# Fixed first tiles of the routed experts, expert bias added at evacuation, and an ordered entry of one-head attention in a graph network kernel

## The chip, the cores and the metric

The kernel runs on one core of a Trainium2 chip. The metric is the device time of the program in microseconds (us). The kernel before takes 2925.66 us, the median of three runs (2923.8, 2925.66 and 2935.31).

## The reference

A graph of 2708 nodes with 256 features passes four layers; each is an attention over the neighbours of the graph (`_gnn`), then a feed-forward part (`_ffn`), both on normalized features and added to `x`.

```
x = x + _L0_gnn_ref(_layernorm(x), adj, ...);  x = x + _L0_ffn_ref(_layernorm(x), ...)
x = x + _L1_gnn_ref(_layernorm(x), adj, ...);  x = x + _L1_ffn_ref(_layernorm(x), ...)
x = x + _L2_gnn_ref(_layernorm(x), adj, ...);  x = x + _L2_ffn_ref(_layernorm(x), ...)
x = x + _L3_gnn_ref(_layernorm(x), adj, ...);  x = x + _L3_ffn_ref(_layernorm(x), ...)
```

Four of these eight parts matter here. `_L1_ffn` sends every node to one of 8 experts (top-1); hidden width 1024:

```
H = gelu(x @ W1 + b1)
probs = softmax(H @ Wg + bg);  assign = argmax(probs)
out[n] = probs[n, assign[n]] * (H[n] @ Wd[assign[n]] + bd[assign[n]])
```

`_L2_gnn` and `_L3_gnn` are attentions with one head (the second adds an elu, the first a bias `W_b`):

```
Wh = h @ W (+ W_b);  f1 = Wh @ a1;  f2 = Wh @ a2
e = leaky_relu(f1[:, None] + f2[None, :], 0.2), -9e15 where adj is 0
out = softmax(e, axis=1) @ Wh
```

`_L2_ffn` is a decoder block: causal attention, then 8 experts of which each node takes two (top-2), `(silu(x @ w1.T) * (x @ w3.T)) @ w2.T`, hidden width 682.

## The kernel before, in words

Nodes lie in 22 tiles of 128 rows (the last has 20), and `X` keeps all of them in on-chip memory. Stages follow one another; most take blocks of 512 nodes, six in all, the last of 148. The order within a stage comes from the order of the code on each engine's queue, and from `issue_after`, which ties an instruction to stand behind another.

**Top-1 experts, `top1_ffn` (L851).** A hidden loop over the six blocks makes H transposed (`hidden`, L900: matmuls at L905, Gelu on ACT), `gate` (L926) makes the routing scores and ranks each node within its expert (`Routing.chunk`, L1322; ranks at L1351, scatter of node numbers into slots by POOL at L1372), and `store` (L912) turns H back to rows (transposes L920, copies L921 by DVE and ACT) and stores each tile to DRAM on SP's queue (L924). `route.finish` (L1382) works out which expert owns which slot. A slot is a tile of 128 places of one expert: in the worst case 29, "usual" 26; slots above the usual number stand under a branch (`others`, L1449). For each slot, SP reads a row number into a register and loads the slot's node numbers, one column of 128 x 4 bytes (L1474); DVE casts them (L962); POOL gathers the rows of H (L964); PE transposes them (L978; copies L979 by DVE and ACT); PE multiplies by the expert's weights, whose number it has read into a register (16 matmuls, L985), and adds the expert's bias by a matmul with K = 8 and a one-hot column (`route.hot`, two instructions, L988); ACT or DVE by turns copies the result (L992), and POOL scatters it to DRAM (L1495). Ahead of slot 0, `prepare` computes the routing weights (`route.weights`) and folds the weights of the coming attention g2 (`Head`, L1033: loads on POOL's queue, products on DVE; L1037, L1045, L1047).

**One-head attention, `gat_single` (L1055)**, runs twice: g2 behind the top-1 experts, g3 behind the decoder. Its entry adds what the experts sent to `X` (`Routing.combine`, a generator by blocks of tiles, DVE), takes mean and variance of each tile (`Stats.sums`, L136: bn_stats and bn_aggr on DVE at L144 and L145, Sqrt on ACT at L146), the reciprocal (L149), normalizes (L108, DVE), transposes on PE (L1098), copies (L1102, ACT), multiplies by W (L123, PE), and forms the exponentials of the scores (L1108, L1109, ACT), the scaled rows V (L1111 ACT and L1113 DVE by turns), a sum of features (L1114, DVE) and the row `big_p` (L1120, ACT). Blocks come in the order 0, 1, 2, then 3 to 5; statistics in three groups: block 0, blocks 1 and 2, blocks 3 to 5. In g2 22 adds of the bias to `X` on POOL (L1149) follow. Then the main loop runs over groups of 768 nodes and 22 tiles j: Relu on ACT (L668), mask on DVE (L669), matmuls (L1168).

**Decoder experts, `experts` (L1761)**, works as the top-1 experts do, with 47 usual slots, of a worst case of 50. SP loads 128 x 258 numbers per slot (f, with the node number in two last columns), again behind a register read; `where` (L1476) works out where a result goes. `inverse_root` (L301), four Newton steps on DVE, serves the decoder's norms.

## Time and profile before

| | before |
|---|---|
| median of three runs | 2925.66 us |
| the profiled execution, its own time | 2935.18 us |
| its span, 33103 instructions | 2933.1 us |
| mean granted TensorE clock | 0.943 |
| busy: PE, DVE, ACT, POOL | 2676.8, 1458.5, 1046.9, 367.2 us |
| hidden loop of the top-1 experts | about 1092 to 1218 us |
| top-1 slots, 26 | 1240.4 to 1376.4 us |
| entry of g2, from its first add to `X` to the main loop | 1384.7 to 1441.9 us |
| decoder slots, 47 | 2198.9 to 2605.7 us |
| entry of g3, likewise | 2613.9 to 2679.4 us |

The span runs from the first to the last instruction of one profiled execution; the execution's own time holds 2.1 us more. Busy time is the sum of an engine's instructions, so an engine at 91% still has waits. Where lines of a view are shown below, "L1168" is line 1168 of the kernel, "acc<-V,e" is output and inputs, "x16" is how many instructions the row puts together, and "<-" in brackets says what ended the idle time before a row.

### The profile page before, as it was taken

How to read it: one execution, taken by the hardware profiler on the slowest of the kernel's cores; microseconds unless marked ns; L12 is line 12 of the kernel's file. 1: busy time of each engine (PE TensorE's matmuls, PEld its weight loads, DVE VectorE, ACT ScalarE, POOL GpSimd, SP SyncE). 2: the span in 40 equal slices, each digit the busy share in tenths (PEclk: the TensorE clock that was granted, in tenths of full speed). 3: DMA queues.
4: the chain of work that ended last, by engine and by line, in shares of the span. 5: the costliest groups of instructions: out<-in, count | busy, mean ns of one | idle time of the engine just before them, and what ended most of it. 6: DMA issues, size and time to landing. Idle time of an engine off the chain costs nothing.

```text
span 2933.1 us, 33103 instructions
## 1 busy us (share of the span) xinstructions
PE 2676.8 (91%) x11945; PEld 1633.7 (56%) x11945; DVE 1458.5 (50%) x3089; ACT 1046.9 (36%) x1605; POOL 367.2 (13%) x464
## 2 busy tenths in 40 slices
PE   6999989799999979797899899999969999969998
PEld 4667646563333325486688433333336676747885
DVE  7743358344777773422644455465543222245455
ACT  3344433225665633211543223233312221224453
POOL 0000012100000001232200123233321111110002
PEclk9999999698999989899999999899959999989999
DMA  8899210000000023443200100002031101041001
GB/s 297 283 293 312 85 64 1 8 0 1 1 1 1 1 85 133 115 130 103 77 1 1 33 22 17 15 2 89 15 109 33 33 30 33 29 151 40 1 1 39
DMA packets 110323, 196.66 MB, mean 67 GB/s; under 512 B 12154, under 2 KB 71034, under 8 KB 107454
## 3 DMA queue, kind: packets, MB, share of 16 engines
q1 hardware_dynamic: 89816, 147.89, 15.6%
q0 software_dynamic: 13360, 38.73, 4.2%
q10 hardware_dynamic: 6986, 7.91, 0.9%
q8 instruction: 100, 1.64, 0.2%
q14 instruction: 61, 0.50, 0.1%
HBM read 134.78 MB, written 59.71 MB: 66 GB/s over the span
## 4 chain that ended last, share of the span: by engine, by line
PE 74%; DVE 10%; DMA 5%; issue 5%; ACT 3%; POOL 2%; ACTq 0%; POOLq 0%; SPq 0%; DVEq 0%
PE acc L1168 15%; PE acc L774 8%; PE acc L278 7%; PE den L782 4%; PE po L1826 4%; PE po L1656 4%; PE sc L1641 3%; PE score L267 3%; DMA f<-hs 3%; PE h L905 3%; PE h L1794 3%; PE pv L123 2%; PE sc L1619 2%; PE po L123 2%; PE y L985 1%
## 5 line engine op out<-in xcount | busy, mean ns | idle before, releaser
L669 DVE SCALAR_TENSOR_TENSOR e<-e,mask 128x768 f32<-128x768 f32 (+2 forms) x264 | 409.5, 1566 | 312.9 <-ACT e L668 312.7
L668 ACT ACTIVATE e<-big_p,minus_one,ratio 128x768 f32<-128x768 f32 (+2 forms) x264 | 394.8, 1513 | 362.8 <-PE acc L1168 229.4
L1168 PE MATMUL acc<-V,e 128*128 128x257 f32 (+1 forms) x1936 | 433.5, 383 | 4.5 <-DVE e L669 2.8
L1168 PEld LDWEIGHTS acc<-V,e 128*128 128x128 f32 (+1 forms) x1936 | 352.2, 186 | 85.8 <-issue 32.1
L774 PE MATMUL acc<-e,V 128*64 128x512 f32 (+1 forms) x1056 | 249.7, 550 | 4.1 <-DVE e L669 4.1
L1794 PE MATMUL h<-w,ft 128*128 x752 | 233.9, 453 | 0.5 <-ACT ft L1783 0.5
L278 PE MATMUL acc<-F,e 128*128 128x257 f32 x968 | 226.3, 384 | 3.0 <-DVE e L275 2.6
L278 PEld LDWEIGHTS acc<-F,e 128*128 128x128 f32 x968 | 173.4, 185 | 67.0 <-DVE e L275 28.4
L774 PEld LDWEIGHTS acc<-e,V 128*64 128x64 f32 x1056 | 95.4, 137 | 180.6 <-issue 158.1
L1641 PE MATMUL sc<-qt,kt 64*128 64x512 f32 (+4 forms) x656 | 185.7, 538 | 4.3 <-ACT e L1651 2.6
L1651 ACT ACTIVATE e<-sc 128x1024 f32<-128x1024 f32 (+4 forms) x140 | 102.7, 760 | 201.1 <-PE sc L1641 177.7
L1794 PEld LDWEIGHTS h<-w,ft 128*128 128x128 f32 x752 | 136.4, 191 | 56.9 <-issue 1.6
L275 DVE TENSOR_TENSOR e<-e,mask 128x512 f32<-128x512 f32 (+2 forms) x132 | 80.5, 625 | 149.2 <-ACT e L269 147.4
L1659 DVE TENSOR_TENSOR sum<-sum,e 128x1024 f32<-128x1024 f32 (+4 forms) x102 | 104.1, 1020 | 97.7 <-ACT e L1651 94.1
L269 ACT ACTIVATE e<-score 128x512 f32<-128x512 f32 (+2 forms) x132 | 69.7, 544 | 179.8 <-PE score L267 153.1
L1656 PE MATMUL po<-e,V 128*64 128x512 f32 (+5 forms) x560 | 119.1, 509 | 14.9 <-ACT e L1651 8.9
L1826 PE MATMUL po<-w,ht 114*128 x564 | 131.2, 382 | 0.9 <-DVE ht L1819 0.9
L1641 PEld LDWEIGHTS sc<-qt,kt 64*128 64x128 f32 x656 | 71.3, 199 | 95.3 <-issue 81.5
L782 PE MATMUL den<-e,low 128*3 128x512 f32 (+1 forms) x1056 | 123.1, 542 | 0.0
L1826 PEld LDWEIGHTS po<-w,ht 114*128 114x128 f32 x564 | 107.9, 191 | 23.1 <-DVE ht L1819 8.2
L1485 DVE TENSOR_SCALAR second<-f,down 128x1 f32<-128x1 f32 x47 | 9.9, 213 | 219.1 <-DMA f<-hs 219.1
L267 PE MATMUL score<-QK 128*128 128x512 f32 (+2 forms) x264 | 112.8, 558 | 1.2 <-ACT e L269 0.7
(600 smaller groups left out, 3554.8 us busy)
## 6 DMA issues: line engine op xcount, KB each, us to landing
row<-in_adj SPq DMA_DIRECT2D x21, 1354.0 KB
raw<-in_adjT SPq DMA_DIRECT2D x35, 768.0 KB
hs<-zero SPq DMA_DIRECT2D x8, 2838.0 KB
hidden<-hr SPq DMA_DIRECT2D x21, 512.0 KB
wd<-in_f_wd SPq DMA_DIRECT2D x8, 1024.0 KB
kept<-mask SPq DMA_DIRECT2D x21, 338.5 KB
mask<-kept SPq DMA_DIRECT2D x21, 338.5 KB
f<-hs SPq DMA_DIRECT2D x47, 129.0 KB
```

The costliest lines, as they stand in the source:

```text
L123: self.nc.tensor.matmul(out, lhsT[:, c, :], rhs[:, c, :], start=first and c == 0, stop=last and c == n - 1)
L267: nc.tensor.matmul(ps[:r, :iw], QK[:, 0, span(j)], QK[:, 1, i0 : i0 + iw], start=True, stop=True)
L278: nc.tensor.matmul(acc[k][:ri], e[:r, k * P : k * P + ri], F[:r, j, :], start=j == 0, stop=j == NT - 1)
L668: nc.scalar.activation(v, big_p[:, i], AF.Relu, bias=net.minus_one, scale=ratio)
L669: nc.vector.scalar_tensor_tensor(v, v, 1.0, net.mask[:, j, i], ALU.add, ALU.mult)
L774: nc.tensor.matmul(acc[n][half, :iw], V[:, j, h, :], e[:, k, i0 : i0 + iw], start=j == 0, stop=j == NT - 1)
L782: nc.tensor.matmul(den[g : g + Q, :iw], low[:, j, h, Q - 1 - q : 2 * Q - 1 - q], e[:, k, i0 : i0 + iw], start=False, stop=j == NT - 1 and ...
L1168: nc.tensor.matmul(acc[k][:ri], e[:, k * P : k * P + ri], V[:, j, :], start=j == 0, stop=j == NT - 1)
L1641: nc.tensor.matmul(ps[:r, g, o:iw], kt[b, span(j)], qt[b, o:iw], start=True, stop=True)
L1656: nc.tensor.matmul(po[b, o:iw], V[:r, j, g, :], e[:r, g, o:iw], start=j == 0, stop=j == last)
L1794: last = nc.tensor.matmul(halves[s, n][:, q, :HALF], fts[s][:, c, :], weights.w13[n][:, bass.ds(es[s], 1), c, q * HALF : (q + 1) * HALF], ...
L1826: last = nc.tensor.matmul(po, ht[:KP, k, :], w2[:KP, bass.ds(es[s], 1), k, :], start=k == 0, stop=k == KC - 1)
```

## The change

It has three parts.

1. *Top-1 experts.* The first tile of each expert is always slot 0 to 7, so those slots need no register; the further tiles follow, and the routing's helper arrays shrink by 8 tiles. One load (`load_first`) brings the node numbers of the first 8 slots, and the other columns are loaded up front. The bias of the experts is broadcast to all partitions by a load of 1 MB on ACT's queue, and DVE adds it while it copies the result; for slots from 8 on, DVE reads the expert's number into a register. `store` of the last-but-one block is kept until the last block has passed its gate; each half of a tile has its own buffer, in a ring of three shared with `q4`, and its own store. `Head` moves from ahead of slot 0 to behind the add of slot 3, its loads to ACT's queue.
2. *Entry of one-head attention.* `turn` puts DVE's steps in an order written out: block 0 alone, then block 1, then further blocks two by two. ACT takes Sqrt for blocks 0 and 1 alone, ahead of the first exponential; the other roots are Newton steps on DVE (`Stats.newton`), now three and not four, which holds for `inverse_root` everywhere. The copy of `ft` becomes two ACT copies that also sum (`accum_out`), in place of DVE's sum at L1114. V is scaled by ACT in blocks 0 to 3, by DVE in blocks 4 and 5. The bias adds of g2 go into the main loop, behind the mask of j = 3.
3. *Decoder experts.* Slots 0 to 7 are fixed likewise, and the routing's `owners`, the weights and `place` follow the first slot's gate.

```diff
-    def sums(self, t0, t1):
+    def sums(self, t0, t1, root=True):
...
-            nc.vector.bn_aggr(self.mv[:r, t, :], st[:r])
-        nc.scalar.activation(self.sd[:, g], self.mv[:, g, 1], AF.Sqrt, bias=net.ln_eps)
+            last = nc.vector.bn_aggr(self.mv[:r, t, :], st[:r])
+        if root:
+            self.root = nc.scalar.activation(self.sd[:, g], self.mv[:, g, 1], AF.Sqrt, bias=net.ln_eps)
+        return last
...
     def roots(self, t0, t1):
-        self.net.nc.vector.reciprocal(self.rstd[:, t0:t1], self.sd[:, t0:t1])
+        return self.net.nc.vector.reciprocal(self.rstd[:, t0:t1], self.sd[:, t0:t1])
...
+    def newton(self, pool, t0, t1):
+        return inverse_root(self.net, pool, self.mv[:, t0:t1, 1], 1.0, LN_EPS, "nr", self.rstd[:, t0:t1])
...
-    for _ in range(4):
+    for _ in range(3):
         nc.vector.scalar_tensor_tensor(t, y, -0.5, y, ALU.mult, ALU.mult)
         nc.vector.tensor_tensor(t, t, x, ALU.mult)
-        nc.vector.scalar_tensor_tensor(y, t, 1.5, y, ALU.add, ALU.mult)
-    return y
+        last = nc.vector.scalar_tensor_tensor(y, t, 1.5, y, ALU.add, ALU.mult)
+    return y if out is None else last
...
-        bd = big.tile([E, D], F32, name="bd")
-        nc.gpsimd.dma_start(bd, a["f1_bd"])
...
-                    hr = rp.tile([P, 2, 512], F32, name="hr", bufs=2)
                     for n, half in enumerate(halves):
+                        hr = rp.tile([P, 512], F32, name="hr", bufs=3)
...
-                    nc.sync.dma_start(rows_of[span(t), :], hr[:r].rearrange("p n m -> p (n m)"))
+                        nc.sync.dma_start(rows_of[span(t), n * 512 : (n + 1) * 512], hr[:r])
...
-            blocks = chunks(512)
+            blocks, kept = chunks(512), []
             ft = features(tiles_of(*blocks[0]))
             for n, (n0, nw) in enumerate(blocks):
                 its = tiles_of(n0, nw)
@@ -947,102 +954,132 @@
                 if n + 1 < len(blocks):
                     ft = features(tiles_of(*blocks[n + 1]))
                 gate(its, halves, nw)
-                store(its, halves)
+                kept.append((its, halves))
+                if n + 2 != len(blocks):
+                    for k in kept:
+                        store(*k)
+                    kept.clear()
...
+            bd = sp.tile([P, E, D], F32, name="bd", bufs=1)
+            nc.scalar.dma_start(bd.rearrange("p e d -> p (e d)"), a["f1_bd"].rearrange("e d -> (e d)").partition_broadcast(P))
...
+            def numbers(group):
+                g = slice(group[0], group[-1] + 1)
+                nc.vector.tensor_copy(number[:, g], node[:, g])
...
+            def places(group):
+                g = slice(group[0], group[-1] + 1)
+                at = sp.tile([P, E], F32, name="at", bufs=2)[:, : len(group)]
+                nc.vector.tensor_tensor(at, node[:, g], route.taken[:, g], ALU.mult)
+                nc.vector.tensor_tensor(to[:, g], at, route.spare[:, g], ALU.add)
...
-                    nc.tensor.matmul(
-                        ps, ht[:, c // 4, c % 4, :], wd[:, bass.ds(experts[s], 1), c, :], start=c == 0, stop=False
-                    )
-                last = nc.tensor.matmul(
-                    ps, route.hot[:E, s : s + 1].to_broadcast([E, P]), bd, start=False, stop=True
-                )
...
+            def expert(engine, s):
+                if s < E:
+                    return slice(s, s + 1)
+                return bass.ds(engine.value_load(route.expert[0:1, s : s + 1], min_val=0, max_val=E - 1), 1)
...
+            route.load_first(node[:, :E])
+            for s in range(E, usual):
+                route.load(s, node[:, s : s + 1])
+            numbers(groups[0])
+            for s in range(4):
+                fetch(s)
+            ready = transposes(0)
+            route.owners()
+            places(groups[0])
+            route.weights(one)
+            heads = []
...
                     with tc.issue_after(last.ins) if last else nullcontext():
-                        experts[s] = nc.tensor.value_load(route.expert[0:1, s : s + 1], min_val=0, max_val=E - 1)
+                        e = expert(nc.tensor, s)
                     this = ready
                     if s + 1 < s1:
                         ready = transposes(s + 1)
-                    last = results(s, *this)
+                    ps = py.tile([P, D], F32, name="y")
+                    for c in range(KC):
+                        last = nc.tensor.matmul(
+                            ps, this[:, c // 4, c % 4, :], wd[:, e, c, :], start=c == 0, stop=c == KC - 1
+                        )
+                    with tc.issue_after(added.ins) if added else nullcontext():
+                        e = expert(nc.vector, s)
+                    y = sp.tile([P, D], F32, name="ys")
+                    added = nc.vector.tensor_tensor(y, ps, bd[:, e, :].rearrange("p e d -> p (e d)"), ALU.add)
+                    route.send(to[:, s : s + 1], y)
+                    with tc.issue_after(added.ins):
+                        for g in groups[1:]:
+                            if s + 6 == g[0]:
+                                numbers(g)
+                                places(g)
+                        if s == 3:
+                            heads.append(Head(net, prep, one, "g2", True, nc.scalar))
                     if s + 4 < s1:
                         fetch(s + 4)
-            heads = []
...
-            through(0, route.usual, prepare)
+            through(0, usual, ready)
...
-        nc.gpsimd.dma_start(w[:, :, :D], a[f"{key}_w"].rearrange("(c p) m -> p c m", p=P))
-        av = net.load_rows(work, a[f"{key}_a"], 2 * D, "av")
+        engine.dma_start(w[:, :, :D], a[f"{key}_w"].rearrange("(c p) m -> p c m", p=P))
...
-                    nc.scalar.copy(ft[:, :, k * P : k * P + pw], ps[:, :, :pw])
+                    for c in range(2):
+                        nc.scalar.activation(
+                            ft[:, c, k * P : k * P + pw],
+                            ps[:, c, :pw],
+                            AF.Copy,
+                            accum_out=parts[:, 2 * n + k // 2, c : c + 1],
+                        )
...
-                        nc.scalar.activation(low, pv[:r, D:], AF.Exp, scale=SLOPE)
+                        with tc.issue_after(ln.root.ins) if t == 0 else nullcontext():
+                            nc.scalar.activation(low, pv[:r, D:], AF.Exp, scale=SLOPE)
                         nc.scalar.activation(ratio[:r, t : t + 1], pv[:r, D:], AF.Exp, scale=1.0 - SLOPE)
-                        if m:
+                        if n < 4:
                             nc.scalar.activation(V[:r, t, :D], pv[:r, :D], AF.Copy, scale=low)
                         else:
-                            nc.vector.tensor_scalar(V[:r, t, :D], pv[:r, :D], low, None, ALU.mult)
-                nc.vector.tensor_reduce(parts[:, n, :], ft[:, :, :nw], AX.X, ALU.add)
+                            with tc.issue_after(last.ins):
+                                nc.vector.tensor_scalar(V[:r, t, :D], pv[:r, :D], low, None, ALU.mult)
...
-            next(rest)
-            stats(0, 0)
-            next(rest)
-            norm(0)
+            def tiles(n0, n1):
+                return tiles_of(*blocks[n0])[0], tiles_of(*blocks[n1])[-1] + 1
+            last = None
+            def turn(step, *args, **kw):
+                nonlocal last
+                with tc.issue_after(last.ins) if last else nullcontext():
+                    new = step(*args, **kw)
+                last = new or last
+            def add():
+                return next(rest, None)
+            turn(add)
+            turn(ln.sums, *tiles(0, 0))
+            turn(add)
+            turn(ln.roots, *tiles(0, 0))
+            turn(norm, 0)
+            turn(ln.sums, *tiles(1, 1))
+            turn(add)
             project(0)
-            next(rest)
-            stats(1, 2)
-            next(rest)
-            norm(1)
+            turn(ln.roots, *tiles(1, 1))
+            turn(norm, 1)
             project(1)
-            next(rest)
-            norm(2)
-            project(2)
-            next(rest)
-            stats(3, 5)
-            for n in range(3, 6):
-                norm(n)
+            turn(ln.sums, *tiles(2, 2), root=False)
+            turn(add)
+            turn(ln.sums, *tiles(3, 3), root=False)
+            turn(ln.newton, small, *tiles(2, 3))
+            for n in (2, 3):
+                turn(norm, n)
                 project(n)
-            if bias:
-                for t in range(NT):
-                    r = rows(t)
-                    nc.gpsimd.tensor_tensor(X[:r, t, :], X[:r, t, :], bias[:r], ALU.add)
+            turn(add)
+            turn(add)
+            turn(ln.sums, *tiles(4, 5), root=False)
+            turn(ln.newton, small, *tiles(4, 5))
+            for n in (4, 5):
+                turn(norm, n)
+            for n in (4, 5):
+                project(n)
             nc.vector.tensor_reduce(fsum, parts.rearrange("p n c -> p c n"), AX.X, ALU.add)
...
-                gat_pairs(net, e, j, i0, iw, big_p, ratio[:, j : j + 1])
+                masked = gat_pairs(net, e, j, i0, iw, big_p, ratio[:, j : j + 1])
+                if bias is not None and i0 == 0 and j == 3:
+                    late = small.tile([P, D], F32, name="late", bufs=1)
+                    with tc.issue_after(masked.ins):
+                        nc.vector.tensor_copy(late, bias)
+                    for t in range(NT):
+                        r = rows(t)
+                        nc.gpsimd.tensor_tensor(X[:r, t, :], X[:r, t, :], late[:r], ALU.add)
...
-            nc.vector.tensor_scalar(n, ps, float(P - 1), None, ALU.add)
+            nc.vector.tensor_scalar(n, ps, 1.0, -1.0, ALU.max, ALU.add)
...
+        if s < self.E:
+            self.loaded = sync.dma_start(f, self.hs[s * CAP : s * CAP + P, :])
+            return
...
+    def load_first(self, f):
+        self.loaded = self.net.nc.sync.dma_start(
+            f, self.hs.rearrange("(e c) d -> c (e d)", e=self.E)[:P, :]
+        )
...
+            if s < E:
+                es[s] = slice(s, s + 1)
+                return
...
             for s in range(s0, min(s0 + 4, s1)):
                 fetch(s)
-            if prepare:
-                route.owners()
             front(s0)
-            if prepare:
-                prepare()
...
             gate(s0)
+            if s0 == 0:
+                route.owners()
+            place(s0)
+            place(s0 + 1)
+            if s0 == 0:
+                shares()
```

## The prediction

> **What bounds the kernel now.** I read the page's engine totals and slices first, then the chain that ended last, then that chain for the stages that the change touches, then windows of the entries.
>
> ```profile
> PE 74%; DVE 10%; DMA 5%; issue 5%; ACT 3%; POOL 2%; ACTq 0%; POOLq 0%; SPq 0%; DVEq 0%
> ```
>
> Over the span PE is 91% busy and carries 74% of the chain: a saving counts where PE has less to do, or where PE waits. The chain for 1160 to 1290 us shows both kinds:
>
> ```profile
> 1217.70 0.56 DVE hr L921
> 1219.72 0.61 PE rank L1351 x2
> ...
> 1223.68 4.20 DMA fnodes<-ftag,fto
> 1228.25 0.53 issue
> 1228.78 0.77 POOL g2w L1037
> 1229.55 2.71 DMA g2bv<-in_g_b
> 1235.65 0.61 DVE bt L1047
> 1236.35 4.04 DMA hr<-hidden,number
> 1240.41 1.94 PE ht L978 x8
> ```
>
> Columns are start, length, what. Between the last hidden block and the first slot of the top-1 experts PE waits about 20 us for a relay: ranks, scatter of node numbers, a DVE that stands for g2's weights, gather. Then PE alone sets the pace:
>
> ```profile
> 1280.26 1.02 PE ht L978 x8
> 1281.29 3.46 PE y L985 x16
> 1284.74 0.62 PE y L988 x2
> 1285.36 1.02 PE ht L978 x8
> ```
>
> A slot is 1.02 + 3.46 + 0.62 = 5.10 us; 26 of them run from 1240.4 to 1376.4. The two entries of one-head attention are mixed. Columns: stretch, length, PE, PEld, DVE, ACT, POOL busy (instructions), granted clock, DMA share, GB/s.
>
> ```profile
> 1384.70:1391.70 7.00, 0.00 (x0) 0.02 (x1) 6.99 (x23) 0.30 (x1) 0.11 (x1) 0.50 0.72 227
> 1391.70:1400.70 9.00, 8.94 (x28) 6.14 (x28) 9.00 (x28) 4.40 (x14) 2.87 (x4) 0.71 0.00 1
> 1400.70:1405.00 4.30, 0.44 (x3) 0.20 (x2) 4.30 (x10) 3.43 (x4) 1.97 (x1) 0.85 0.08 10
> 1405.00:1414.00 9.00, 8.69 (x26) 5.98 (x27) 8.91 (x22) 2.99 (x12) 5.81 (x8) 0.69 0.47 150
> 1414.00:1420.70 6.70, 6.32 (x29) 4.65 (x28) 6.30 (x21) 6.01 (x14) 2.47 (x4) 1.00 0.48 150
> ```
> ```profile
> 2636.00:2640.00 4.00, 1.39 (x6) 0.51 (x4) 4.00 (x14) 3.68 (x7) 0.00 (x0) 0.92 1.04 406
> 2654.20:2657.20 3.00, 0.06 (x1) 0.06 (x2) 2.23 (x12) 2.18 (x3) 0.00 (x0) 0.87 0.01 3
> 2657.20:2666.30 9.10, 9.10 (x28) 6.85 (x29) 4.88 (x12) 4.23 (x13) 0.00 (x0) 0.67 0.00 0
> 2666.30:2673.00 6.70, 6.41 (x30) 4.69 (x29) 2.10 (x3) 3.43 (x14) 0.00 (x0) 1.00 0.01 2
> ```
>
> PE waits 7 us for block 0, about 4 us for block 1 (behind DVE), and in g3 again 3 us for block 3. A block costs 6.7 us at clock 1.00 and 9.0 at 0.7.
>
> **1. Expert bias.** The matmul pair at L988 goes: 26 x 0.62 = **16.1 us**, all on the chain. In its place DVE adds a broadcast bias while it evacuates, in every slot (before: copies of 0.42 us on DVE, 0.37 on ACT, by turns), and reads the expert number into a register in 18 slots. No DVE register load is in the trace. Nearest is SP's: its node loads come every 1.09 us with 0.33 of that the issue, so 0.76 us; DVE then does 0.69 (ht copy) + 0.42 + 0.76 = 1.9 us per 4.48-us slot. It binds only above 4.48 - 1.11 - about 0.5 of waiting = 2.9 us. Behind the load stand the bias add and the next ht copy, for which PE waits. I take nothing; bounds 0 to 3 us lost. A gain is excluded, since nothing leaves PE but L988. POOL has 2.56 us per slot (two indirect DMAs at 0.97 to 0.99, two gaps of 0.30), also below 4.48.
>
> **2. Dispatch.** Stores of block 4 are put behind block 5's gate, so ranks come earlier by that block's four tiles of transposes and copies: their two groups take PE and the copies about 6.4 us, from the stretch between the last hidden matmul and L1351. The scatter then lands near 1222.5 instead of 1227.9. What is late next is SP: ten half-row stores in a ring of three, about 1.07 us each, the last near 1225.3, and the node load stands behind them in SP's queue. It is now one load of 128 x 8 numbers. The Trainium skill, "DMA: Bandwidth & Descriptors", rules for kernel authors, warns that a strided last dimension becomes one descriptor per element: 1024 pieces where one column had 128, a reason against. The trace prices such pieces: from 1228.2 to 1240.3 us the hardware queue moved 1160 small packets in 4.7% of 16 engines' time, 12.1 x 0.047 = 0.57 us. So 1024 cost about 0.5 us beyond the landing time; as an upper bound I take the issues of the eight column loads that it replaces, 8 x 0.33 = 2.6. I take 0.5, the row of the same pieces. The 1 MB bias broadcast, moved to ACT's queue here, could hold it up by 0 to 3 us (1 MB at the 340 GB/s of nearby slices); I take 1. So the numbers arrive near 1228.5, DVE's weights (softmax behind an Exp table load of 1.28 at 1219.44) end near 1228.8, number near 1229; first gather to first PE took 5.4 us (1235.03 to 1240.41), so PE starts near 1235: **5 us** (2 to 8).
>
> The 4.60-us DVE wait for g2's bias goes. Head's folding, about 4.0 us of DVE, moves to behind slot 3's add with its DMAs on ACT's queue. There the ht copy of slot 5 is done some 5.3 us after that add and PE needs it at 5.5: free, but close. Without this cover up to 4 us once.
>
> **3. Hidden loop.** Each tile's two halves share a ring of three buffers. A half's copy 0.69, store issue 0.33, landing about 2 and hand-overs 0.2 make 3.2 us per three halves, 1.07 each, against 8.5 us per 8 halves of PE and copy, 1.06: just at the edge. I take **1.5 us lost** over the five full blocks (0 to 6).
>
> **4. g2's entry** (57.2 us from the first X add at 1384.71 to the main loop at 1441.9). Block 0's sums go first and alone: add 4 x 0.41, sums 4 x 0.43, Sqrt with its load 1.58, reciprocal 0.18, first normalization: PE at +5.65 instead of +7.0. The 22 bias adds leave POOL; beside them DVE's L108 took 0.85 each in block 1's window against 0.345 in g3. They go into the main loop, where 22 x 0.74 = 16 us of POOL lie beside six times as much PE work; DVE has 0.96 us in a j of 2.60, so even doubled it is covered.
>
> Two of three Sqrts go (DVE's Newton steps take their place): two loads of 1.28 and 0.30 each, 5.7 us of ACT per entry. "ScalarE: Activation LUTs", what ACT_TABLE_LOAD costs, adds a drain of about 1.38 us to each load, 2.66 in all, which would make four loads 10.6 us instead of 5.1. Here the following ACTIVATE starts 0.01 us after the load (1400.58 + 1.28, then 1401.87), so I take the row. Against it ACT gets more: sums by accumulating copies, four of (0.42 + 0.19, from the row of the same form at L1686) for two of 0.58, and all V scalings in blocks 0 to 3. Per block ACT has 2.4 + 4 x 0.24 (the added passes) + 4 x 0.47 + 0.69, about 6.1 us, against PE's 6.67: not over it, but each pair's copy stands in PE's way, about 0.7 us per block. So 5.65, two blocks of 9.0 at the low clock, three of 7.35, and the last stretch of 6.6 as now: main loop at +52.3. With one hand-over of DVE uncovered (2 to 3 us) it is +55. I take +54: **3 us** (-2 to +7).
>
> **5. g3's entry.** Its first Sqrt waits for mask transfers queued ahead on ACT (table load at 2626.39 after 20.26 us idle); their order is kept, so PE still starts near 2629. The two waits go (2636 to 2640: 2.6 us, 2654.2 to 2657.2: 2.9), and block 3 may stay warm. "TensorE: Matmul & The Clock Gate", part 1, halves the clock after an idle window of some 3.4 us; here a 3.0-us gap was followed by 9.1 us at 0.67 against 6.7. By the row closing the gap is worth 2.4 us more, by the rule nothing is sure at 3.0. I count it: 2.6 + 2.9 + 2.4, less six bubbles of 0.7, is 3.7; rounded down for the clock, **3 us** (0 to 6).
>
> **6. Decoder.** The first loads need no register: they were issued at 2195.06, 1.6 us after the row numbers (L1407, 2193.51), and can now go at 2193.4: **1.6 us** (0 to 3). Its 47 slots of 8.14 us keep their PE work. One Newton iteration less in the send: three steps of 0.2 = **0.6 us**.
>
> Sum: 16.1 + 5 - 1.5 + 3 + 3 + 1.6 + 0.6 = 27.8 us. Against the profiled execution, 2935.18 (span 2933.1, 2.1 outside it), that is 2907.4. That execution is 9.5 us above the median of the runs, 2925.66; no row says where those 9.5 us lie, so I take the same saving from both, and the median becomes 2925.66 - 27.8 = **2898**.
>
> **Rivals.**
> - *Only the matmuls count* (0.18). Accumulating copies make ACT the bound of the entries (6.1 of 6.7 us speaks for it), and dispatch waits for stores. Then 16.1 + 2.2 - 1.5, about 17: 2909.
> - *Warm entries* (0.12). Without gaps PE keeps clock 1.00 in blocks 1 to 5 of both entries, where 9.0-us blocks stand now: 2 x 2 blocks x 2.3 = 9, and the dispatch at its best, 3 more: 2886. Against it: the clock starts at 0.50 in any case.
> - *Gain given back* (0.08): ring and dispatch at their bad ends, -6 and 0, Head's 4 us bare, entries nothing: 16.1 + 2.2 - 6 - 4 = 8: 2917, within the 0.5% (14.6 us) that a measurement of this kernel can tell from no change.
> - *Slower* (0.04): the DVE register load in 18 slots sets the slot. It begins to bind at 2.9 us; each further us costs 18. From 2.9 + 28/18 = 4.5 us all is eaten; at 5.5 us, 18 x 2.6 = 47 lost against 28: 2945. Speaks for it: it sits between PE's result and the next copy, and reads memory. Against: SP's 0.76.
>
> The rest, 0.58, is the forecast, 2888 to 2908. Faster 0.88 (all but the last two), same 0.08, slower 0.04. The range goes from the warm case to the upper end of "only the matmuls", 2881 to 2914.
>
> **What would show it.** Slots: pitch 4.48 and no L988; 5.1 or more says DVE or POOL set it. Dispatch: first transpose of slot 0 about 18 us instead of 23 after the last hidden matmul of block 5. Hidden loop: period still 22.67 us per block. Entries: 52 to 55 us in g2, one Sqrt group at the start, no PE gap over 1 us after block 1; blocks of 8 us would mean that ACT sets the pace. Decoder slots 8.14. I am wrong if the slots don't shrink by 0.6, or if the entries grow.

## The result and the profile after

The changed kernel takes 2897.7 us (median of four runs, 2889.25 to 2900.03) against 2927.35 for the kernel before, run beside it: a ratio of 0.9894 with an interval of 0.9868 to 0.9921, 23 to 39 us. The forecast was 2898. Its sum is another matter: of its terms, one has the wrong sign, and others make up for it.

The two profiled executions differ by 38.7 us (2896.45 against 2935.18; spans 2894.7 and 2933.1). That is 9 us more than the medians: the profiled execution of before is 7.8 us above its median, that of the changed kernel 1.3 below. Both spans are divided at the same events. Lengths in us, from the starts of the instructions named (the two slot stages to the end of their last matmul):

| stage | before | after | difference | prediction |
|---|---|---|---|---|
| start of the hidden loop to slot 0's first transpose | 144.9 | 152.6 | +7.7 | -5 + 1.5 |
| top-1 slots, to the last matmul | 136.0 | 116.1 | -19.9 | -16.1 |
| g2, first add to `X` to the main loop | 57.2 | 49.1 | -8.1 | -3 |
| g3, likewise | 65.5 | 58.2 | -7.3 | -3 |
| last score of the decoder's attention to its experts' first matmul | 36.0 | 31.9 | -4.1 | -2.2 |
| decoder slots | 405.6 | 401.4 | -4.3 | 0 |
| from g2's main loop to the decoder's last score | 722.2 | 718.4 | -3.8 | 0 |
| all else | 1365.7 | 1367.1 | +1.4 | 0 |

**Dispatch.** Rows of the timeline of after, with what ended the idle time before each in brackets:

```profile
1214.46 0.40 PE L1423 MATMUL rank<-fone,fbefore 128*128 128x16 f32 x2 [0.29 <-DVE fone L1403]
...
1222.43 0.69 DVE L927 COPY hr<-hr 128x512 f32<-128x512 f32 x1 [3.61 <-DMA hidden<-hr]
1226.10 0.59 ACT L927 COPY hr<-hr 128x512 f32<-128x512 f32 x1 [7.84 <-DMA hidden<-hr]
1228.11 0.69 DVE L927 COPY hr<-hr 128x512 f32<-128x512 f32 x1 [3.98 <-DMA hidden<-hr]
...
1234.23 0.41 SPq L1554 DMA_DIRECT2D node<-fnodes  x1
1234.25 0.39 ACTq L968 DMA_DIRECT2D bd<-in_f_bd  x1
...
1241.48 0.17 DVE L980 CAST number<-node 128x8 int32<-128x8 f32 x1 [6.20 <-DMA node<-fnodes]
...
1242.54 1.00 POOL L990 DMA_INDIRECT hr<-hidden,number  x1 [23.00 <-DMA node<-fnodes]
...
1247.79 0.45 PE L1003 MATMUL ht<-ident,hr 128*128 128x128 f32 x1 [17.05 <-DMA node<-fnodes]
```

The ranks come at 1214.5, 5.3 us earlier than before, near the forecast. But from 1222.4 on, copies into the ring wait for a store to land. The last store is issued at 1231.8. SP and ACT issue the loads of node numbers and bias together at 1234.2; SP's view of waits shows what the first of them waited for (us in total, times, longest):

```profile
SPq L1554 <- DMA hidden<-hr: 1.5, 1, 1.5
```

It is the landing of a store. From that issue to their use by DVE the numbers need 7.2 us. Against before, the 7.7 us are: the load issued 6.3 us later, 0.9 more from its issue to the cast, 0.6 more from the cast to the first gather, 0.1 less from there to PE.

**Slots.** Two slots of the timeline of after:

```profile
1295.30 1.04 PE L1003 MATMUL ht<-ident,hr 128*128 128x128 f32 x8
1295.50 0.42 DVE L1041 TENSOR_TENSOR ys<-y,bd 128x256 f32<-128x256 f32 x1 [2.87 <-PE y L1035]
...
1296.17 3.62 PE L1035 MATMUL y<-wd,ht 128*128 x16
...
1299.62 1.04 PE L1003 MATMUL ht<-ident,hr 128*128 128x128 f32 x8
```

From transposes to transposes, the pitch of a slot, it is 4.33 us, and was 5.10. After slot 1's transposes PE waits for no other engine in these slots, while DVE stands idle 2.87 us ahead of its add. All pitches but the first and the last are 4.33, those behind slot 3 too, so the folding of g2's weights found cover, as predicted.

**Entries.** Windows of after; columns as in the prediction. In g2 the first row ends with PE's first transpose, the next two together hold blocks 0 and 1, and each further row holds one block. g2:

```profile
1372.56:1378.28 5.72, 0.00 (x0) 0.03 (x1) 5.68 (x20) 0.30 (x1) 0.00 (x0) 0.50 0.83 264
1378.28:1383.70 5.42, 5.42 (x16) 4.20 (x17) 5.38 (x20) 2.65 (x8) 0.00 (x0) 0.51 0.00 2
1383.70:1395.32 11.62, 10.05 (x42) 6.87 (x41) 11.17 (x45) 7.91 (x35) 0.00 (x0) 1.00 0.00 0
1395.32:1401.92 6.60, 6.33 (x29) 4.63 (x28) 6.08 (x30) 4.86 (x21) 1.80 (x1) 1.00 0.30 90
1401.92:1408.52 6.60, 6.33 (x29) 4.63 (x28) 1.64 (x6) 4.87 (x21) 0.00 (x0) 1.00 0.50 152
```

g3, whose first two rows hold blocks 0 and 1:

```profile
2597.50:2603.90 6.40, 5.25 (x17) 4.02 (x17) 6.36 (x22) 3.91 (x15) 0.00 (x0) 0.64 0.98 350
2603.90:2614.30 10.40, 10.00 (x41) 6.76 (x41) 9.96 (x41) 6.58 (x31) 0.00 (x0) 1.00 1.04 403
2614.30:2620.90 6.60, 6.60 (x29) 4.62 (x30) 6.60 (x19) 4.88 (x21) 0.00 (x0) 1.00 0.10 35
2620.90:2627.40 6.50, 6.32 (x30) 4.62 (x29) 5.98 (x30) 4.77 (x21) 1.35 (x2) 1.00 0.23 61
```

Blocks from the third on take 6.5 to 6.6 us at clock 1.00. ACT is busy for at most 4.9 us in each, so it has room.

### The profile page after: what moved, and what is told of

Same layout as the page of the kernel before. It is cut to its first block, busy times and chain, and to the rows that moved or that the text cites. A ratio compares the mean times of both kernels' runs of the same rounds, so it can differ in the third digit from the quotient of the medians.

```text
span 2894.7 us, 32765 instructions
## 1 busy us (share of the span) xinstructions
PE 2651.2 (92%) x11893; PEld 1624.4 (56%) x11893; DVE 1441.4 (50%) x3062; ACT 1041.2 (36%) x1658; POOL 369.5 (13%) x462
## 3 DMA queue, kind: packets, MB, share of 16 engines
q1 hardware_dynamic: 92758, 147.89, 16.1%
## 5 line engine op out<-in xcount | busy, mean ns | idle before, releaser
L1878 PE MATMUL h<-w,ft 128*128 (+1 forms) x752 | 233.0, 452 | 0.5 <-ACT ft L1860 0.5
L1878 PEld LDWEIGHTS h<-w,ft 128*128 128x128 f32 x752 | 136.0, 191 | 56.7 <-issue 1.4
L1910 PE MATMUL po<-w,ht 114*128 (+1 forms) x564 | 129.5, 379 | 0.9 <-DVE ht L1903 0.9
```

Source lines behind the costliest of these rows:

```text
L1878: last = nc.tensor.matmul(halves[s, n][:, q, :HALF], fts[s][:, c, :], weights.w13[n][:, es[s], c, q * HALF : (q + 1) * HALF], start=c == 0 ...
L1910: last = nc.tensor.matmul(po, ht[:KP, k, :], w2[:KP, es[s], k, :], start=k == 0, stop=k == KC - 1)
```

## The experiments

The theory after the result: the bias pair costs more than its own 0.62; dispatch is later through two waits, the stores put behind the gate and the broadcast ahead of the node numbers; the entries gain from DVE's order and from the absent table switches. All kernels start from the changed one. Stages as in the table above, from one profile each (us), the time as a median where it is not one run:

| kernel | time | hidden loop to slot 0 | slots | g2 | g3 | decoder slots |
|---|---|---|---|---|---|---|
| before | 2927.4 | 144.9 | 136.0 | 57.2 | 65.5 | 405.6 |
| after | 2897.7 | 152.6 | 116.1 | 49.1 | 58.2 | 401.4 |
| bias by matmul | 2915.3 | 146.9 | 135.2 | 49.2 | 57.1 | 400.5 |
| stores at once | 2893.4 | 145.3 | 116.4 | 49.2 | 59.7 | 406.2 |
| no broadcast | 2899.5 | 146.6 | 117.5 | 48.3 | 58.3 | 401.6 |
| entry as before | 2911.8 | 151.4 | 116.8 | 57.1 | 66.4 | 403.0 |
| bias on POOL | 2895.2 (one run) | 151.3 | 115.1 | 48.9 | 58.2 | 402.9 |
| sums by DVE | 2889.7 (one run) | 151.4 | 114.9 | 48.4 | 61.8 | 402.4 |
| Sqrt by ACT | 2907.3 (one run) | 151.2 | 114.9 | 54.9 | 59.2 | 400.9 |
| place behind the gate | 2882.1 | 150.7 | 115.2 | 49.1 | 58.2 | 390.0 |
| broadcast late | 2892.7 (one run) | 147.4 | 117.2 | 48.0 | 58.3 | 402.9 |
| all three mends | 2872.0 | 143.4 | 115.2 | 49.1 | 59.7 | 388.5 |

The table also shows how far a stage differs between profiles in which no edit touches it: 150.7 to 152.6 for the way to slot 0, 114.9 to 117.5 for the slots, 48.0 to 49.2 in g2, 57.1 to 59.7 in g3, 400.5 to 406.2 in the decoder's slots. A smaller difference than that says nothing. For the way to slot 0 the changed kernel's own profile is the longest, so what a kernel below gains there on it may be up to 1.9 us too large.

### Bias by matmul

```diff
-                            ps, this[:, c // 4, c % 4, :], wd[:, e, c, :], start=c == 0, stop=c == KC - 1
+                            ps, this[:, c // 4, c % 4, :], wd[:, e, c, :], start=c == 0, stop=False
...
+                    last = nc.tensor.matmul(
+                        ps, route.hot[:E, s : s + 1].to_broadcast([E, P]), bd, start=False, stop=True
+                    )
...
-                    added = nc.vector.tensor_tensor(y, ps, bd[:, e, :].rearrange("p e d -> p (e d)"), ALU.add)
+                    new = (nc.scalar.copy if s % 2 else nc.vector.tensor_copy)(y, ps)
```

> The changed kernel with the bias matmul pair back in every top-1 slot, results copied by ACT and DVE in turns, no expert number read by DVE, and no broadcast of the bias (1 KB is loaded, not 1 MB). By the theory that the pair cost more than its own 0.62 us on the chain (the pitch fell from 5.10 to 4.33), the pitch returns to 5.10: 25 x 0.77 = 19 us more in the slots. By the rival (0.62 each, the rest from something else in the slots, such as the copies that no longer go by turns) it is about 4.95: 16 us. If the broadcast also held up the load of the node numbers ahead of slot 0, the first transposes come 3 to 4 us earlier than the changed kernel's 38.9 us after the hidden loop; if not, at the same 38.9. Sum: about 2913 by the first with the broadcast in the way, 2917 without.

2915.3 us, a ratio to before of 0.9965 (0.9953 to 0.9977). The pitch is 5.10 again and the slots take 19.2 us more: the pair's price is 0.77 per slot. Starts of single matmuls in the traces say where the 0.15 beyond 0.62 lies: the first matmul of the pair starts 0.309 us after the one before it where all others follow at 0.216, and the second transpose behind the pair 0.165 after the first, where the rest follow at 0.109. Slot 0 comes 5.7 us earlier without the broadcast (this kernel loads 8 KB of bias, not the 1 KB of the expectation), and the numbers need 3.0 us.

### Stores at once

```diff
-                kept.append((its, halves))
-                if n + 2 != len(blocks):
-                    for k in kept:
-                        store(*k)
-                    kept.clear()
+                store(its, halves)
```

> The changed kernel with the stores of block 4 where they were, ahead of block 5's gate; all else as changed, the ring of three half-row buffers too. By the theory that putting ten stores behind the gate moved the end of the last store, and with it the load of node numbers, to 1234 us: the time from the end of the hidden loop's start to slot 0 falls by 5 to 7 us (slot 0 near 1241 to 1243), 2891 to 2893 in all. By the rival that the ring of three itself holds the stores up, the hidden loop gets longer by what the dispatch gets shorter, and slot 0 stays within 2 us of 1247.8: 2897.

2893.4 us (0.9868 of before, 0.9839 to 0.9898); slot 0 comes 7.3 us earlier. The hidden loop takes 117.8 us to its last matmul, as in before (117.7), with the ring of three in place: the ring costs nothing there. So the rival falls. In its timeline the numbers, loaded beside the broadcast, still need over 7 us from their load to the cast:

```profile
1225.34 0.40 SPq L1550 DMA_DIRECT2D node<-fnodes  x1
...
1232.81 0.17 DVE L976 CAST number<-node 128x8 int32<-128x8 f32 x1 [6.26 <-DMA node<-fnodes]
```

### No broadcast

```diff
-            nc.scalar.dma_start(bd.rearrange("p e d -> p (e d)"), a["f1_bd"].rearrange("e d -> (e d)").partition_broadcast(P))
+            nc.gpsimd.memset(bd, 0.0)
```

> The changed kernel with the 1 MB broadcast of the expert bias left out: POOL fills the buffer with zeros (so the bias's values are left out). By the theory that the broadcast stood in the way of the node numbers, their load falls from 7.2 us to 3 to 4 us and slot 0 begins 3 to 4 us earlier: 2894. By the rival that the 1024 single numbers of the load are slow by themselves, it stays at 7 us and the time at 2897.

The numbers take 4.0 us, not 7.2, and slot 0 comes 6.0 us earlier:

```profile
1233.23 0.41 SPq L1554 DMA_DIRECT2D node<-fnodes  x1
...
1237.21 0.17 DVE L980 CAST number<-node 128x8 int32<-128x8 f32 x1 [2.82 <-DMA node<-fnodes]
```

The rival falls too: the same 1024 numbers are quick without their neighbour. In all seven profiles with the broadcast beside them they need 7.2 to 7.5 us, in the four without it 3.0 to 4.0. Of the 6.0 us, 3.3 are this load; 1.7 are an earlier issue, which seven other kernels with the same stores have too (1.2 to 2.2 us).

The stage speaks for the theory; the total does not show it: 2899.5 (0.9898, 0.9876 to 0.992), like the changed kernel, where 2894 was expected. In this profile the decoder's attention took 495 us where the changed kernel's took 486; more on that below.

### Entry as before

`gat_single` of the kernel before, whole.

> The changed kernel with the entry and main loop of one-head attention as before (three Sqrt groups, copies without sums, DVE's reduction, bias adds on POOL). By the theory that the new entry alone made both entries shorter, g2's goes from 49.1 back to 57 us and g3's from 58.2 back to 65.5: 15 us more, about 2913. By the rival that part of it came from what precedes (the bias's loads, the state of the clock), less than 10 us comes back.

2911.8 us (0.9943, 0.9922 to 0.9964), 14.1 more than after; the entries go back to 57.1 and 66.4, together 16.1 more. The gain belongs to the entries' own code.

### Bias on POOL, sums by DVE, Sqrt by ACT

```diff
+            if bias is not None:
+                for t in range(NT):
+                    r = rows(t)
+                    nc.gpsimd.tensor_tensor(X[:r, t, :], X[:r, t, :], bias[:r], ALU.add)
```

(the adds in the main loop go.)

> The changed kernel with g2's 22 bias adds on POOL back in its entry, ahead of the main loop. If POOL beside DVE was what slowed the normalizations and the entry (prediction, step 4), g2's entry grows from 49.1 by 2 us or more, and g3's, which has no bias, stays at 58.2. If the order of DVE's steps made the difference, g2's stays within 1 us of 49.

```diff
-                        nc.scalar.activation(
...
-                            accum_out=parts[:, 2 * n + k // 2, c : c + 1],
...
+                    nc.scalar.copy(ft[:, :, k * P : k * P + pw], ps[:, :, :pw])
...
+                nc.vector.tensor_reduce(parts[:, n, :], ft[:, :, :nw], AX.X, ALU.add)
```

> The changed kernel with one ACT copy per pair of tiles and DVE's reduction of 1.2 us per block in place of the accumulating ACT copies. By the prediction's reckoning the accumulating copies cost each block some 0.7 us on PE's path: without them the entries would be 2 to 4 us shorter. By the rival, that ACT has room and DVE has none in blocks 0 to 3, the entries get longer by 1 to 5 us.

```diff
-            turn(ln.newton, small, *tiles(2, 3))
+            act_root(*tiles(2, 3))
+            turn(ln.roots, *tiles(2, 3))
```

(likewise for blocks 4 and 5; `act_root` is the Sqrt on ACT.)

> The changed kernel with Sqrt by ACT for blocks 2 and 3 and for blocks 4 and 5 in place of DVE's Newton steps: two table loads of 1.28 and a Sqrt of 0.30 come back for each, 5.7 us of ACT per entry, while DVE loses 12 steps of 0.2 twice. If the table switches stood on the path of the old entries, each entry grows by 3 to 6 us; if only the order mattered, it stays within 1 us of 49.1 and 58.2.

By stages, as the single totals hide it (the decoder's attention took 478 us with sums by DVE, 495 with Sqrt by ACT): with POOL's adds g2's entry takes 48.9 us, no longer than without. Yet they do slow DVE beside them. The normalizations of 21 tiles in g2's entry, with POOL's adds and without (busy us, mean ns, idle us before):

```profile
L108 DVE TENSOR_SCALAR f<-X,mv,rstd 128x256 f32<-128x256 f32 x21 | 12.5, 660 | 0.2
```
```profile
L108 DVE TENSOR_SCALAR f<-X,mv,rstd 128x256 f32<-128x256 f32 x21 | 7.1, 408 | 0.2
```

In the new order those 5.4 us of DVE are off PE's path. What they cost in the old order no run shows.

Sums by DVE leave g2 as it is (48.4) and make g3 3.5 longer; the accumulating copies are no burden in either. Sqrt by ACT makes g2 5.8 longer; in g3, where 3 to 6 were expected too, the 1.0 lies within the differences between profiles. For g2 the view of waits, a stretch of the timeline and two windows of that kernel show how:

```profile
PE pv L123 <- ACT ft L1140: 5.0, 4, 2.5
```
```profile
1395.97 1.28 ACT L1186 ACT_TABLE_LOAD   x1
1397.26 0.30 ACT L1186 ACTIVATE sd<-mv,ln_eps 128x6 f32<-128x6 f32 x1
1397.58 1.28 ACT L1153 ACT_TABLE_LOAD   x1
...
1398.99 0.39 ACT L1140 ACTIVATE ft<-tp 128x256 f32<-128x256 f32 x1
...
1399.53 2.94 PE L123 MATMUL pv<-g2w,ft 128*128 128x257 f32 x6 [2.55 <-ACT ft L1140]
```
```profile
1387.10:1396.40 9.30, 7.97 (x29) 5.78 (x30) 7.17 (x26) 6.28 (x26) 1.80 (x1) 0.82 0.19 58
1396.40:1406.70 10.30, 7.75 (x31) 5.68 (x30) 2.21 (x7) 7.37 (x27) 0.00 (x0) 0.83 0.46 145
```

Copies of ft stand behind the table switches, PE waits four times, 2.5 us at most, and the clock falls to 0.82 and 0.83 in two stretches of a block's length. From the end of one block's score matmuls (L1162) to the next's, blocks 1 and 2 take 10.35 and 10.29 us, and 6.59 and 6.60 in after; the last block gives some of it back. In g3 the sums undone give back 3.5 of the 8.2 us that the whole entry undone gives. The rest stays open: the order itself no run took alone.

### Place behind the gate

The decoder's slots were 4.3 us shorter, which nothing in the prediction foresaw. In the changed kernel the first slots have a pitch of 8.16, the middle ones about 8.48, the last mostly 8.15; in before all but the last six had about 8.54. A middle slot of after:

```profile
2405.66 0.33 SPq L1550 DMA_DIRECT2D f<-hs  x1
...
2407.66 0.21 DVE L1563 TENSOR_SCALAR second<-f,down 128x1 f32<-128x1 f32 x1 [5.26 <-DMA f<-hs]
2407.91 0.27 DVE L1566 TENSOR_SCALAR second<-second,f,dhas 128x1 f32<-128x1 f32 x1
2408.21 0.16 DVE L1567 TENSOR_TENSOR to<-second,dspare 128x1 int32<-128x1 f32 x1
2408.29 0.87 DVE L1895 TENSOR_TENSOR hh<-hh,h 128x682 f32<-128x682 f32 x1
2409.21 0.87 PE L1902 MATMUL pt<-ident,hh 128*114 128x128 f32 x6
```

DVE waits for a load that was issued 2.0 us earlier, and the gate (L1895) stands behind it. PE waits for that gate, in the middle slots of after (first row) and, as the prediction had not seen, of before:

```profile
PE pt L1902 <- DVE hh L1895: 7.2, 31, 0.5
```
```profile
PE pt L1818 <- DVE hh L1811: 9.2, 34, 0.5
```

```diff
-                        place(s + 2)
...
-                gate(s + 1)
+                gated = gate(s + 1)
+                if s + 2 < s1:
+                    with tc.issue_after(gated.ins):
+                        place(s + 2)
```

> The changed kernel with one edit in the decoder's slots: the three small DVE steps of slot s + 2 that need its loaded numbers (place) are tied behind the gate of slot s + 1. In the changed kernel they stand ahead of it and wait for a load, 2.0 us after its issue, and PE waits for the gate, 0.3 us in 34 slots; slots without that load have a pitch of 8.15, the others 8.48. If that wait makes the difference, nearly all slots go to 8.15: 34 x 0.33 = 11 us less in the decoder, 2886 in all. If it is the register reads of PE, the pitch stays at 8.48 and the time at 2897.

2882.1 us (0.9847, 0.9831 to 0.9864). All slots but the first (8.14) and the last (7.93) now have 8.15 or 8.16, with PE's register reads as they were, so the rival falls; the decoder's slots lose 11.4 us. PE no longer waits for the gate. Its rows, no longer behind a load:

```profile
2392.25 0.86 DVE L1895 TENSOR_TENSOR hh<-hh,h 128x682 f32<-128x682 f32 x1 [5.64 <-PE h L1878]
2393.03 0.21 DVE L1563 TENSOR_SCALAR second<-f,down 128x1 f32<-128x1 f32 x1
2393.17 0.87 PE L1902 MATMUL pt<-ident,hh 128*114 128x128 f32 x6
```

### Broadcast late, and all three mends

```diff
             ready = transposes(0)
+            with tc.issue_after(held["copy"].ins):
+                nc.scalar.dma_start(bd.rearrange("p e d -> p (e d)"), a["f1_bd"].rearrange("e d -> (e d)").partition_broadcast(P))
```

(`held["copy"]` is the ACT copy of slot 0's transposes.)

> The changed kernel with only the bias broadcast moved behind the first copy of slot 0's transposes. If the broadcast ahead of the node numbers was the wait, their load takes about 4 us, as with no broadcast at all, and slot 0 comes 6 us earlier after the hidden loop (146.6 us from its start, not 152.6); the slots stay at 116 us, or take up to 4 us more if the addition now waits. If the other loads (g2's weights) are what counts, it stays at 152.

One run, 2892.7 us: slot 0 comes 5.2 us earlier, and the numbers need 4.0 us. The slots take 1.2 longer, which lies within the differences between profiles.

> The changed kernel with three edits at once: stores of block 4 where they were, the bias broadcast issued behind the first copy of slot 0's transposes, and the decoder's place behind its gate. If the three waits are separate, the parts add: 7.3 us from the stores (as the run with stores at once showed), about 4 us from the node numbers' load (7.5 to 3.5), 10.3 us in the decoder: 2897.7 - 21.6 = 2876. If the broadcast, now beside the first gathers, delays slot 0's addition, the slots grow by up to 4 us: 2880.

2872.0 us (0.9815 of before, 0.9796 to 0.9834), the fastest, and 25.7 less than the changed kernel. The decoder gives 12.9 us where 10.3 were expected, the numbers take 3.95 us from load to cast, and slot 0 comes 9.2 us earlier than in after, not 11.3. The load is issued 1.5 us later than with stores at once, behind the landing of the last scatter of node numbers (SP's wait, 1.1 us). From the start of the hidden loop to slot 0 it is 143.4 us, 1.5 less than before: even so mended, the dispatch doesn't give the 5 us of the prediction.

## Why the number was right and the sum was not

**Bias (step 1): right, too small.** The term was 26 x 0.62 from the chain's row. The row holds the time that the chain gives to L988; it leaves out what the pair does to its neighbours. Measured: 25 distances of 0.77, 19.3 us. That nothing takes the pair's place was right. DVE's register read (shortest, median and longest in ns) was this:

```profile
L1011 DVEq TENSOR_LOAD <-fexpert x18: 300/304/551, 1287.0 to 1360.4; - x18
```

With 0.19 and 0.02 behind it that is about 0.5 us, under the 0.76 that I had taken from SP, and DVE still had 2.87 us of idle time. With that the rival of a slower kernel fell.

**Dispatch (step 2): wrong, +7.7 instead of -3.5 with step 3.** The early ranks came as predicted; two estimates behind them failed. The first is "ten half-row stores in a ring of three, about 1.07 us each, the last near 1225.3": the last was issued at 1231.8. The term in it that failed is the landing of a store, which I had set at about 2. With three buffers each copy needs the store of the copy three before it to have landed. That holds for the first of these stores, issued at 1211.75: its buffer was written again at 1213.91, 2.2 us later. Of these two

```profile
1214.52 0.32 SPq L930 DMA_DIRECT2D hidden<-hr  x1
...
1217.00 0.32 SPq L930 DMA_DIRECT2D hidden<-hr  x1
```

the buffers were free for the copies at 1222.43 and 1226.10 only, 7.9 and 9.1 us later. What holds the stores up stays open; POOL's six scatters of node numbers (1212.3 to 1219.5) run beside them. Then the load of the numbers waits for a store to land as well, which the prediction had not counted. The run with stores at once gave 7.3 us back.

The second is the broadcast, at "0 to 3 us; I take 1": with it the numbers need 7.2 us from load to cast, without it 4.0, so it costs 3.3, a little over the upper end. What the 1024 single numbers cost by themselves is not shown, since no run loads the first eight columns one by one; the loss that "DMA: Bandwidth & Descriptors" warns of can be no more than a part of the 3.0 to 4.0 us in the four runs without the broadcast beside the load.

The "23" us from the last hidden matmul to slot 0 are a misreading: in before they are 27.2 (1213.23 to 1240.41), and 38.9 in after.

**Hidden loop (step 3): no loss.** 117.8 us with the ring of three and stores at once, 117.7 before.

**g2 and g3 (steps 4 and 5): right in kind, mis-sized.** The first PE work came at +5.72 (5.65 predicted). The failed term is "each pair's copy stands in PE's way, about 0.7 us per block". PE waits 0.27 us for a copy in a block, and the 6.67 that I set as PE's own held such waits already: in the prediction's own row of a 6.70-us block PE is busy for 6.32. Blocks now take 6.5 to 6.6 us. ACT's sum of 6.1 us per block was too high, since 4.9 are measured. Against the +54 of the prediction, three blocks of 7.35 took 6.6 (2.3 us), the first two 17.0 and not 18.0 (1.0), and the uncovered hand-over was not there (1.7): 5.0, where 4.9 are missing (49.1 for 54). In g3 the six bubbles were 4.2 us, and 4.3 are missing. The clock is 1.00 from 1383.7 on in g2 and from 2603.9 on in g3; so the entries did what the rival "warm entries" said (9 us more than the forecast, measured 9.4), and that was given a chance of 0.12.

Table switches: by the row two of them cost 5.7 us of ACT per entry, with the drain that "ScalarE: Activation LUTs" gives 11 us. In the rows above ACT is held from 1395.97 to 1398.86, 2.9 us for one Sqrt, and starts each activation 0.01 to 0.02 us after a load: the row holds. That g2 then grew by 5.8 us, almost the same number, is chance: PE's time went into waits for copies and a lower clock. The bias on POOL, to which step 4 had given a share, had none in the new order, though it slows DVE as read there.

**Decoder (step 6): right, too small.** The entry gained 4.1, not 2.2. The first load was issued 2.4 us earlier after attention's last score, near the 2.2 of the prediction. The other 1.7 are the load: from its issue to PE's first transpose it is 2.2 us (2168.60 to 2170.82) and was 3.9 (2195.06 to 2198.95); two loads of POOL were then ahead of it, at 2193.80 and 2194.57, which no run tried apart. The slots' "8.14 us" was read from the last six; most of the 47 had 8.54, with the wait for the gate in them. Six pitches of 8.16 in the fixed slots, whose loads come early enough for `place`, are 2.3 of the 4.3 us; the rest lies within the differences between profiles.

So the 11.2 us missed in dispatch were made up by 3.8 in the bias, 5.1 and 4.3 in the entries, and 1.9 and 4.3 in the decoder, 19.4 together: 36.0 for the profiled pair in the stages edited, and 38.4 with attention and the rest. The runs' medians differ by 29.7; the forecast of 27.8 met that with errors that cancel, which is luck. How the 9 us between the pair and the medians divide is not settled; the decoder's attention, below, differs by more than that from run to run, but by only 1.6 us in this pair.

## What to carry to other kernels

A small matmul with few rows between big ones can cost its neighbours too: price it by the pitch with and without it, not by its own row. A step moved out of the critical wait is not free in the queue that it lands in: ask what is behind it on DVE and SP, how long its transfer takes to land there, and which other transfer runs beside the one that ends the wait. An engine with 50% busy time can still hold PE up in every slot, when a step that waits for a load stands ahead of the one that PE needs.

## What the runs showed of the hardware

The decoder's attention, which no edit touches, took 478 to 495 us in these profiles, in step with the granted clock. Its windows, with sums by DVE and with Sqrt by ACT:

```profile
1648.48:2126.85 478.37, 444.88 (x1865) 174.91 (x1864) 254.84 (x502) 145.52 (x229) 138.34 (x111) 0.96 0.07 25
```
```profile
1655.77:2150.94 495.17, 462.28 (x1866) 183.30 (x1864) 253.88 (x502) 146.34 (x229) 140.27 (x113) 0.92 0.07 25
```

PE's busy time goes from 444.9 to 462.3 us with the mean clock, 0.96 and 0.92; ACT and DVE change by less than 1 us. So single totals of this kernel differ by up to 17 us for a reason outside the edit, and stage lengths tell more than totals. What sets the clock there stays open.

The clock also fell to 0.82 in g2 with Sqrt by ACT. "TensorE: Matmul & The Clock Gate", part 1, gives an idle window of some 3.4 us for that; the gaps of PE there are 2.55 us at most. But between its gaps PE ran transposes only: from the end of one group of multiplications by W (L123) to the next it is 3.4 us, both times (1385.75 to 1389.19, 1396.10 to 1399.53). Whether transposes count as work for the clock, no run tried, so these runs don't decide against the page.
